# Reordering the first loads of a gated-recurrence layer, with fewer warm-up passes on TensorE

## The chip, the cores and the metric

The kernel runs on one core of one Trainium2 chip. The metric is the device time of one execution in microseconds (us); three runs of the kernel before gave 619.55, 619.95 and 620.02, median 619.95. Engines are named as in the profile: PE is the matrix engine (TensorE), with its weight loads shown apart as PEld; DVE is VectorE, ACT is ScalarE, POOL is GpSimd, and SP (SyncE) issues most of the DMAs. A suffix q (SPq, ACTq) marks an instruction of the engine's sequencer, such as the issue of a DMA.

## The reference

The input `x` has eight sequences of 1024 tokens with 256 channels. Each is normalized, goes through two branches, and both are added to it:

```python
xn = _layernorm(x)
# branch 1: gated linear recurrence, 384 channels
gate, u = xn @ Wg.T, xn @ Wi.T
y  = causal_depthwise_conv4(u) + conv_b
ig = sigmoid(y @ lru_Wi.T + lru_bi);  rg = sigmoid(y @ lru_Wg.T + lru_bg)
alpha = exp(-8 * softplus(lam) * rg);  beta = sqrt(1 - alpha**2 + 1e-6)
h  = associative_scan(h = alpha * h_before + beta * ig * y)
a  = (gelu(gate) * h) @ Wo.T
# branch 2: token-shifted feed-forward, 256 channels
xr, xk = mu * xn + (1 - mu) * xn_before      # one mu for r, one for k
f  = sigmoid(xr @ W_r.T) * (square(relu(xk @ W_k.T)) @ W_v.T)
out = x + a + f
```

Everything is float32.

## The kernel before

One sequence after the other goes through the core. A sequence is eight tiles of 128 tokens (`TT = 8`). Most products are done by a seven-product scheme of Strassen and Winograd: for it GpSimd forms sums of weight blocks (`weight_sum`, L408, tiles `sum_u`, `sum_k` and so on, once for the whole kernel) and sums of token blocks (`token_sum`, L803, tiles `xsum`, `side`, `rsum`, `ysum`, for every sequence). The products themselves are recorded at L415 (512 columns) and L421 or L830 (by token).

The order of instructions on every engine is written out by hand. `steps` collects calls with a due time, either given or from the table `PLACES`, and at the end they are issued in the order of these times. Nothing reorders them after that: each engine works through its own queue in order, and waits at an instruction until the semaphores that it needs are there. The head of the program, lines L1002 to L1087, stands ahead of that and is issued as written.

What the head does, in the order in which the steps follow from each other:

- The loads. SP issues `xt` (x of the first sequence) as four DMAs of two tiles each, 256 KB (`load`, L707). ACT issues the weights of u, `w_i`, 384 KB (`load_weight`, L349), then the parameters `par` (L1010), and loads its table for Sqrt (L1011). SP goes on with the other weights: `w_g` for the gate, which lies in the same tile `w_u`, then `w_k`, `w_r`, `lru_wg`, `lru_wi`, `w_v`, `w_o`.
- The DMAs of SP and ACT share eight semaphores in turn. A DMA waits until the one issued eight places before it has landed.
- `busy(15)`: fifteen matmuls on zeros (L1025, 128x512, bf16) that nothing reads. PE can do nothing else until they are through, since its queue is in order.
- Normalization of tiles 0 and 1: `sums_of_tiles` (L725) and `moments` (L729) on DVE, `deviation` (L732) on ACT, `inverse` (L739, L740) on DVE, and `normalize`, one tile on ACT (L749) and one on DVE (L747).
- `early_transposes(0)` (L1044): four transposes of 128x128 on PE into one bank; `early_put(0)` (L1057): ACT copies the bank into `xnT`. Then `busy(2)`, two more matmuls on zeros.
- The same for tiles 2 and 3, 4 and 5, 6 and 7, interleaved with the first products. These are u's first two row blocks, done plainly in quarters of 256 tokens (`plain_quarters`, L581): quarter f needs `xnT` of tiles 2f and 2f+1, so PE alternates between transposes of the next pair and products of the last.
- ACT's queue has `early_put(0)` ahead of `deviation` of tiles 2 and 3, so that deviation waits until PE has done the first transposes.
- POOL starts `weight_sum` for `sum_u` when `w_i` and `w_g` have landed, does the sums for r and k after it, and then the token sums of `xnT`, `xk` and `xr`.

After the head comes u's second group, then k, r, v and so on, each as seven products; the other seven sequences follow with PE as the engine that is always busy.

Of the kernel before, what the change touches and what calls it, by code (L numbers as in the profile page):

```python
# [9 lines left out]
AF = mybir.ActivationFunctionType  # L10
# [231 lines left out]
def kernel(  # L242
# [24 lines left out]
    nc = tc.nc  # L267
    B, S, D = x.shape
    TT = S // P
# [6 lines left out]
    def fixed(name, shape, dtype=F32):  # L276
        return const.tile([P] + shape, dtype, tag=name, name=name)


    par = fixed("par", [COLS])  # L280
# [57 lines left out]
    def take():  # L338
        return free.pop(0)

    def give(b):
        free.append(b)
# [4 lines left out]
    def load_weight(engine, name, src):  # L347
        family, first = ROWS[name]
        engine.dma_start(families[family][:, :, first * P : first * P + src.shape[2]], src)  # L349
# [356 lines left out]
    def load(s, t, n):  # L706
        nc.sync.dma_start(  # L707
            xt[:, t : t + n, :],
            x[s, t * P : (t + n) * P, :].rearrange("(t p) d -> p t d", p=P),
        )  # L710
# [8 lines left out]
    def stats(s, t, n):  # L719
        sums_of_tiles(s, t, n)  # L720
        moments(s, t, n)
# [279 lines left out]
    with tc.manual_schedule():  # L1001
# [1 line left out]
        nc.gpsimd.memset(ln_eps, LN_EPS)  # L1003
        nc.gpsimd.memset(beta_eps, BETA_EPS)
        make_identity(nc, ident)
        for t in range(0, TT, 2):
            load(0, t, 2)
            if t == 2:
                load_weight(nc.scalar, "i", w_i)
                nc.scalar.dma_start(par, params)  # L1010
                nc.scalar.preload_act_table(AF.Sqrt)  # L1011
        load_weight(nc.sync, "g", w_g)
        load_weight(nc.sync, "k", w_k)
        load_weight(nc.sync, "r", w_r)
# [7 lines left out]
        def busy(n):  # L1022
            for _ in range(n):
                b = take()
                nc.tensor.matmul(banks[b], warm[:, 0:P], warm, start=True, stop=True)  # L1025
                give(b)
# [40 lines left out]
                mu_rest, par[:, COL_MU_R : COL_MU_K + DC], -1.0, 1.0, ALU.mult, ALU.add  # L1067
            )

        busy(15)  # L1070
        stats(0, 0, 2)
        scales(0, 2)
        early_normalize(0)
# [289 lines left out]
```

## Time and profile before

| What | Value |
|---|---|
| Median of three runs | 619.95 us |
| The profiled execution's own time | 620.45 us |
| Its span, first to last instruction | 618.7 us |
| PE busy | 613.3 us (99%), 2539 instructions |
| DVE, ACT, POOL busy | 532.0, 472.7, 320.2 us (86%, 76%, 52%) |
| PE busy from 0 to 20 us | 18.07 us |
| PE busy from 20 to 200 us, and from 200 to 600 us | 179.60 us, 400.00 us |
| PEld idle in the first 20 us, by what ended it | ACT `xnT` (put) 1.4 us, `xt` (normalize) 1.7 us |

The profile is of one execution. A row of the timeline gives the start in us from the span's start, the duration in us, the engine, the line, the operation, the tiles and, in brackets, how long the engine stood idle before it and for whom. A row of the chain of waits gives a start, a duration and what held the program up then: the chain is followed back from the last instruction, at each step to what released it. "issue" is time in which an engine waited for nothing that the profile shows.

### The profile page before, as it was taken

The numbers are of one execution on the slowest core, as the hardware profiler recorded it, in microseconds if no ns is written. First come the engines' busy times: TensorE is split into PE (matmuls) and PEld (weight loads), VectorE is DVE, ScalarE is ACT, GpSimd is POOL, SyncE is SP. The second block draws the span as 40 slices with busy tenths as digits, with TensorE's granted clock in tenths as the row PEclk, the third lists the DMA queues.
The fourth block names the chain that finished last, engine by engine and source line by source line (L and its number), as shares of the span: only waits on it lengthen the run. The fifth ranks groups of instructions, "written<-read, shape, count | busy, mean of one in ns | idle before, by whom it ended". The sixth has DMA issues, their size and how long they took to land.

```text
span 618.7 us, 7488 instructions
## 1 busy us (share of the span) xinstructions
PE 613.3 (99%) x2539; PEld 370.0 (60%) x2539; DVE 532.0 (86%) x659; ACT 472.7 (76%) x671; POOL 320.2 (52%) x227
## 2 busy tenths in 40 slices
PE   8999999999999999999999999999999999999998
PEld 4575445954469544794448844497445964457466
DVE  5789799999989798898899888998888986789696
ACT  4988998668894788938889398884888749884880
POOL 4977923579034950549407492084911769427000
DMA  7200600164001810029000480006500044000403
GB/s 272 69 1 8 129 0 1 27 179 69 0 1 48 195 31 0 1 69 205 0 1 1 102 171 0 2 3 151 120 0 1 17 120 69 0 0 1 69 17 119
DMA packets 35478, 35.10 MB, mean 57 GB/s; under 512 B 2800, under 2 KB 34928, under 8 KB 35440
## 3 DMA queue, kind: packets, MB, share of 16 engines
q1 hardware_dynamic: 26416, 25.63, 14.9%
q0 software_dynamic: 8320, 8.39, 9.1%
q10 hardware_dynamic: 704, 0.60, 0.3%
q8 instruction: 20, 0.33, 0.2%
q14 instruction: 18, 0.15, 0.1%
HBM read 19.94 MB, written 8.39 MB: 46 GB/s over the span
## 4 chain that ended last, share of the span: by engine, by line
PE 96%; DVE 3%; issue 0%; ACT 0%; DVEq 0%
PE bank L415 65%; PE bank L421 24%; PE bank L830 4%; PE bank L1025 1%; PE bank L581 1%; DVE xr L820 1%; DVE xt L747 0%; DVE bank L499 0%; DVE st L725 0%; PE bank L754 0%; DVE q L915 0%; PE bank L1044 0%; DVE mv L740 0%; DVE q L930 0%; DVE mv L729 0%
## 5 line engine op out<-in xcount | busy, mean ns | idle before, releaser
L415 PE MATMUL bank<-y,w_l 128*128 128x512 f32 x288 | 138.2, 593 | 0.1
L898 DVE SCALAR_TENSOR_TENSOR y<-u,par,y 128x1024 f32<-128x1024 f32 x72 | 111.6, 1573 | 0.2
L491 ACT COPY bank<-bank 128x512 f32<-128x512 f32 x76 | 43.8, 576 | 61.3 <-PE bank L415 45.3
L415 PEld LDWEIGHTS bank<-y,w_l 128*128 128x128 f32 x288 | 52.9, 190 | 59.2 <-issue 56.9
L499 DVE TENSOR_TENSOR bank<-bank,five 128x512 f32<-128x512 f32 x76 | 52.3, 689 | 26.4 <-PE bank L415 25.6
L415 PE MATMUL bank<-ysum,sum_l 128*128 128x512 f32 x144 | 71.1, 594 | 0.2
L415 PE MATMUL bank<-xsum,sum_u 128*128 128x512 f32 x138 | 69.3, 592 | 0.0
L803 POOL TENSOR_TENSOR tr<-g 128x512 f32<-128x512 f32 x12 | 22.0, 1836 | 83.7 <-ACT u L611 69.8
L803 POOL TENSOR_TENSOR ysum<-y,ysum 128x512 f32<-128x512 f32 x16 | 28.4, 1777 | 53.6 <-DVE y L898 51.1
L803 POOL TENSOR_TENSOR xsum<-ysum 128x512 f32<-128x512 f32 x12 | 16.0, 1347 | 66.0 <-PE bank L421 58.8
L415 PEld LDWEIGHTS bank<-ysum,sum_l 128*128 128x128 f32 x144 | 26.8, 190 | 35.3 <-issue 28.7
L496 ACT COPY five<-bank 128x512 f32<-128x512 f32 x76 | 43.6, 583 | 4.9 <-PE bank L415 2.9
L415 PE MATMUL bank<-xnT,w_u 128*128 128x512 f32 x92 | 47.0, 592 | 0.0
L623 ACT ACTIVATE tr<-bank,half_b 128x512 f32<-128x512 f32 x48 | 32.0, 679 | 15.6 <-PE bank L415 15.6
L415 PEld LDWEIGHTS bank<-xsum,sum_u 128*128 128x128 f32 x138 | 25.7, 190 | 29.7 <-issue 27.5
L421 PE MATMUL bank<-w_o,g 128*128 128x128 f32 x288 | 37.0, 275 | 0.0
L623 ACT ACTIVATE ti<-bank,half_b 128x512 f32<-128x512 f32 x48 | 31.5, 683 | 7.1 <-PE bank L415 6.9
L421 PEld LDWEIGHTS bank<-w_o,g 128*128 128x128 f32 x288 | 35.0, 192 | 2.9 <-issue 2.9
L749 ACT ACTIVATE xt<-xt,mv,std 128x256 f32<-128x256 f32 x60 | 33.9, 596 | 1.5 <-DVE mv L740 1.5
L922 DVE SCALAR_TENSOR_TENSOR ti<-ti,y 128x1024 f32<-128x1024 f32 (+1 forms) x25 | 29.9, 1216 | 3.9 <-ACT ti L623 3.9
L803 POOL TENSOR_TENSOR ysum<-y 128x512 f32<-128x512 f32 x16 | 20.4, 1273 | 23.8 <-DVE y L898 20.1
L925 DVE SCALAR_TENSOR_TENSOR ti<-ti,q 128x1024 f32<-128x1024 f32 (+1 forms) x25 | 31.8, 1272 | 0.7
(165 smaller groups left out, 1480.3 us busy)
## 6 DMA issues: line engine op xcount, KB each, us to landing
side<-in_x_dram POOLq DMA_DIRECT2D x8, 1024.0 KB, 9.3
xt<-in_x_dram SPq DMA_DIRECT2D x28, 256.0 KB, 5.1
xnT<-xk SPq DMA_DIRECT2D x96, 64.0 KB, 2.0
out_dram<-side SPq DMA_DIRECT2D x12, 512.0 KB, 4.8
xt<-in_x_dram SPq DMA_DIRECT2D x1, 1024.0 KB, 5.3
out_dram<-side SPq DMA_DIRECT2D x4, 256.0 KB, 2.2
out_dram<-side SPq DMA_DIRECT2D x6, 128.0 KB, 1.8
w_l<-in_lru_wg_dram SPq DMA_DIRECT2D x1, 576.0 KB, 5.8
```

The costliest lines, as they stand in the source:

```text
L415: nc.tensor.matmul(banks[b], weight, tokens, start=start, stop=True, skip_group_check=True)
L421: nc.tensor.matmul(banks[b][:, p], tokens[:, p], weight, start=start and j == 0, stop=True, skip_group_check=True,)
L491: nc.scalar.copy(banks[bank["B"]], banks[bank["A"]])
L496: nc.scalar.copy(self.five, banks[bank["C"]])
L499: nc.vector.tensor_tensor(banks[bank["C"]], banks[bank["B"]], self.five, ALU.add)
L623: nc.scalar.activation(dst[:, m, HALVES[h]], src, AF.Tanh, bias=half_b[:, b + m : b + m + 1], scale=0.5)
L749: nc.scalar.activation(xa, xa, AF.Identity, bias=m, scale=r)
L803: nc.gpsimd.tensor_tensor(dst[o], a, b, ALU.subtract)
L830: nc.tensor.matmul(banks[b][:, j * D : (j + 1) * D], lhs[:, c, (t + j) * P : (t + j + 1) * P], families[w][:, c, :], start=(j == 0 and c = ...
L898: nc.vector.scalar_tensor_tensor(y[:, m, :], u[:, m, k : k + S], column(COL_CONV_W + k * HC + m), y[:, m, :], ALU.mult, ALU.add,)
L922: nc.vector.scalar_tensor_tensor(ti[:, m, p], ti[:, m, p], 1.0, y[:, m, p], ALU.add, ALU.mult)
L925: nc.vector.scalar_tensor_tensor(ti[:, m, p], ti[:, m, p], 0.5, q[:, m, p], ALU.mult, ALU.mult)
```

## The change

In the head, all loads but the parameters go to SP. Tiles 0 and 1 come as two DMAs of 128 KB in place of one of 256 KB, the weights `w_i` of u come third, then the three other pairs of tiles, then the other weights in the order that they had. ACT loads its Sqrt table first and issues the parameters after that. The warm-up passes ahead of the first transposes become eleven in place of fifteen; the two after the transposes stay.

```diff
-        for t in range(0, TT, 2):
+        nc.scalar.preload_act_table(AF.Sqrt)
+        load(0, 0, 1)
+        load(0, 1, 1)
+        load_weight(nc.sync, "i", w_i)
+        for t in range(2, TT, 2):
             load(0, t, 2)
-            if t == 2:
-                load_weight(nc.scalar, "i", w_i)
-                nc.scalar.dma_start(par, params)
-                nc.scalar.preload_act_table(AF.Sqrt)
+        nc.scalar.dma_start(par, params)
         load_weight(nc.sync, "g", w_g)
         load_weight(nc.sync, "k", w_k)
         load_weight(nc.sync, "r", w_r)
...
-        busy(15)
+        busy(11)
         stats(0, 0, 2)
         scales(0, 2)
         early_normalize(0)
```

Nothing else differs. The engines' queues keep their order from the first transposes on; the banks that the products use are shifted by four places, and the semaphores of the DMAs by one.

## The prediction

> **What bounds the kernel now.** I read the page first: PE is busy 99% of the span.
>
> ```profile
> PE 613.3 (99%) x2539; PEld 370.0 (60%) x2539; DVE 532.0 (86%) x659; ACT 472.7 (76%) x671; POOL 320.2 (52%) x227
> ```
>
> In the stretches, PE is busy 400.00 us of 200 to 600 and 18.07 us of 0 to 20. So a gain in the head counts as far as PE's continuous run begins earlier, and no other engine then comes late for it. Next I read the chain of waits of the first 60 us.
>
> ```profile
> 1.18 5.96 PE bank L1025 x15
> 7.14 0.45 PE bank L1044 x4
> ...
> 8.10 0.31 ACT std L732
> ...
> 8.82 0.98 DVE xt L747
> ...
> 10.70 0.94 DVE mv L740
> 11.64 0.16 DVE mv L729 x2
> 11.79 1.06 DVE xt L747
> 12.85 0.04 issue
> 12.90 0.55 PE bank L1044 x3
> 13.44 1.81 PE bank L581 x8
> 15.25 0.44 PE bank L1044 x4
> 15.69 2.67 PE bank L581 x12
> 18.36 13.73 PE bank L415 x32
> ```
>
> The reader should see three stretches: the warm-up passes hold the start to 6.98 (where the first transpose begins), then a chain of DVE and ACT for normalizing holds PE until 12.90, and from there PE runs without a gap through the plain quarters to 18.36. Last, the timeline of DVE, ACT and POOL.
>
> ```profile
> 5.22 0.41 DVE L747 TENSOR_SCALAR xt<-xt,std,mv 128x256 f32<-128x256 f32 x1
> 5.96 0.75 DVE L725 BATCH_NORM_STATS2 st<-xt 128x6 f32<-128x256 f32 x2 [0.33 <-DMA xt<-in_x_dram]
> 6.85 0.72 DVE L725 BATCH_NORM_STATS2 st<-xt 128x6 f32<-128x256 f32 x2
> ...
> 5.22 0.60 ACT L749 ACTIVATE xt<-xt,mv,std 128x256 f32<-128x256 f32 x1 [0.43 <-DVE mv L740]
> ...
> 8.65 2.01 POOL L408 TENSOR_TENSOR sum_u<-w_u 128x384 f32<-128x384 f32 x2 [7.21 <-DMA w_u<-in_w_g_dram]
> 10.62 0.99 POOL L408 TENSOR_TENSOR sum_u<-sum_u,w_u 128x384 f32<-128x384 f32 x1
> 11.70 1.00 POOL L408 TENSOR_TENSOR sum_u<-w_u,sum_u 128x384 f32<-128x384 f32 x1
> ```
>
> Tiles 0 and 1 are ready at 5.22 + 0.60 = 5.82, so the transposes wait 1.16 us for warm-ups. And DVE's 256-wide operations, 0.41 us at 5.22, take 0.98, 0.94 (a 2-wide one, 0.16 at 5.02) and about 1.1 us once POOL runs: each ends 0.03 to 0.14 us after an operation of POOL ends (9.66, 11.61, 12.70). While POOL runs, such an operation costs what is left of POOL's.
>
> **The change, step by step.** *Four passes fewer.* Weight loads of warm-ups start every 0.43 us up to 6.27, then at 6.55 and 6.76: the twelfth starts at 5.85. After eleven, the transposes can start at 5.85 in place of 6.98: 1.13 us earlier, hidden by nothing, since the data is there at 5.82. But the pitch falls to 0.21 only at about 6.4, so PE's clock has not risen when the eleven are through; the four transposes, 0.60 us before, may take up to twice that, and I take 0.25 us more.
>
> [...]
>
> *The loads.* By the packet records of the trace, the order in which bytes moved was already x0-1, w_i (first packet at 2.69, though ACT issued it at 0.73), x2-3 (mostly from 3.7), and the new order is the same. One SP issue of 256 KB takes 0.5 us, of 384 KB 0.69 (w_g). So after: tile 0 at 0.73, tile 1 at about 1.2, w_i at about 1.7, x2-3 at 2.4, x4-5 at 2.9, x6-7 at 3.4, w_g at 3.9 where it was 2.75. From issue to first packet the first load took 1.1 us (0.73 to 1.82), so w_i can move at 2.8 and x2-3 at 3.5: I expect the landings to stay (x0-1 3.40, w_i 5.23, x2-3 5.94, x4-5 6.73, x6-7 7.46, w_g 8.51), within -0.4 to +0.7 us; the far end is w_g's issue-to-landing of 5.8 us with its issue 1.1 us later, half of it made up. Two single tiles land tile 0 up to 0.4 us earlier, worth nothing while the eleven passes last until 5.85; if tile 1 came 0.4 us later, that cover would be gone and it would cost the excess.
>
> The later SP issues are all behind more than 2 us of queued bytes. `w_k` waits for tile 0's landing, `lru_wi` for `par`; `par` (first read at 13.64, landed at 6.15) may be 0.6 us later: nothing. ACT's table load of 1.28 us moves from 2.06 to 0.73, nothing, since ACT's first use is at 4.49.
>
> *What follows on the chain.* ACT's put of pair 0 (7.62) comes at 6.75; the next deviation can start at 7.2 (8.10). DVE is through the sums of tiles 4 and 5 at 6.85 + 0.72 = 7.57, so the reciprocal starts at 7.6 (8.43), and DVE's normalization of tile 3 at 8.0, ahead of POOL's start at 8.65, so it takes 0.41, not 0.98: end 8.41 (9.80), with ACT's tile 2 at 8.6 (9.42). The second transposes go at 8.65 (9.48, held up to 9.86). Sums of tiles 6 and 7 and a reciprocal (0.87 us by the row of 9.73 to 10.59) put the 2-wide `mv` operation at 9.30 (10.70). It ends with POOL's first operation, at 9.7 (11.64); normalization of tile 5 ends with POOL's second, at 10.75 (12.84). So the third transposes are ready at 10.75; PE has the second transposes (0.44), two quarters (8 x 0.223 = 1.78, with put 1 through at 9.86) until 10.87. From there it needs 5 quarters x 0.892 + 2 x 0.44 = 5.35 us: the quarters end at 16.2, where they ended at 18.36. Normalization of tile 7 ends with POOL's fourth operation, 12.84 at worst, and is wanted at 13.1.
>
> That is 2.1 us. *Does it reach the end?* POOL's weight sums still start at 8.65 and end at 15.69; the first token sum takes 1.30, so it is there at 17.0, where PE now wants it at 16.2 + 0.86 = 17.1 (17.69 and 19.05 before). POOL is 0.7 us earlier, PE 2.1: all later deliveries of POOL lose 1.4 us of slack. They have: 2.2 (second sum, 20.31 against 22.5), 2.2 (`side`, 23.76 against 25.92), 2.0 and more to 33.3, where POOL itself waited 1.23 us for DVE, which follows PE. The tightest is `rsum` at 36.73 against 37.15. I take 0.1 us off for such places: a gain of 2.0 us. On the profiled execution, 620.45 - 2.0 = 618.45; that lies 0.50 above the median, so against the median 617.95.
>
> **The rivals.** *One POOL slot missed (gain 1.0).* If the chain is 0.36 us later, the `mv` operation misses the end of POOL's first operation at 9.66 and ends at 10.65, and tile 5 at 11.75; PE's run starts at 11.9 in place of 12.9: 618.95. For it: the second `mv` before did just that. [...] Against: 0.36 us of margin.
>
> *The loads come later (no gain).* If x2-3 lands 0.65 us later, DVE's tile 3 starts after POOL's 8.65 and ends at 9.80 as before; the rest is as before: 619.95. For it: SP now issues what two queues did, and x2-3's issue moves from 1.23 to 2.4. Against: x2-3's packets moved from 3.7 only.
>
> [...]
>
> *It does not do what it says:* moving w_i to SP does nothing for its landing; I hold that likely and it is in the sum.
>
> **The numbers.** Full gain (617.5 to 618.5): 0.55. One slot missed (618.6 to 619.3): 0.27. No gain: 0.10. Slower: 0.08. A measurement of this kernel tells 0.2% from no change, about 1.24 us, so faster means below 618.71 and slower above 621.19. The first case and a quarter of the second are faster: 0.62; most of the slower case stays within 0.2%, so slower 0.05, same 0.33. The range from 617.4 to 619.4 takes in the first two cases.
>
> **What would show it.** First transposes (L1044) at 5.8 to 5.9; the third group at 10.8 to 11.0 (one slot missed: 11.9); the first L415 at about 16.2; warm-up pitch, and whether L581 passes come at 0.22 or 0.45 us; POOL's first weight sum at 8.6 to 8.8; no new PE wait for `xsum` at 17 or for `rsum` at 35. I am wrong if POOL starts after 9.4, if the sums of tiles 2 and 3 start after 6.5, or if PE gains in the head and gives it back at a POOL delivery.

## The result, and the profile after

The changed kernel takes 622.04 us (median of six runs, 621.22 to 622.97) where the kernel before takes 619.59 (six runs beside it, 619.29 to 620.02): a ratio of 1.0039, 95% interval 1.0029 to 1.0049. The change loses 2.45 us where 2.0 were forecast to be won. The profiled execution took 622.67 us, span 620.9. The six runs lie in two groups: three at 621.22 to 621.41, where TensorE's mean granted clock is 1.000, and three at 622.67 to 622.97, where it is 0.997.

Timeline of PE in the kernel after (start, duration, what; in brackets the idle time before and for whom):

```profile
5.86 1.06 PE L1045 MATMUL bank<-ident,xt 128*128 128x128 f32 x4
8.92 0.66 PE L1045 MATMUL bank<-ident,xt 128*128 128x128 f32 x4 [0.20 <-ACT xt L749]
11.22 0.60 PE L1045 MATMUL bank<-ident,xt 128*128 128x128 f32 x4
...
16.57 1.02 PE L415 MATMUL bank<-xnT,w_u 128*128 128x512 f32 x2
19.84 1.12 PE L415 MATMUL bank<-xsum,sum_u 128*128 128x512 f32 x2 [2.25 <-POOL xsum L803]
20.80 1.86 PE L415 MATMUL bank<-xnT,w_u 128*128 128x512 f32 x2
22.45 1.91 PE L415 MATMUL bank<-xsum,sum_u 128*128 128x512 f32 x2
24.15 1.08 PE L415 MATMUL bank<-xnT,w_u 128*128 128x512 f32 x2
25.07 1.02 PE L415 MATMUL bank<-xsum,sum_u 128*128 128x512 f32 x2
```

The reader should see two things. Up to 16.57 the change does what was forecast: the first seven-product multiplication (L415) starts 1.62 us earlier than before (18.19). Then PE does one pair of products and stands idle for 2.25 us, since POOL has not delivered `xsum`. Before, the same two pairs followed each other without a gap:

```profile
18.19 1.02 PE L415 MATMUL bank<-xnT,w_u 128*128 128x512 f32 x2
19.05 1.02 PE L415 MATMUL bank<-xsum,sum_u 128*128 128x512 f32 x2
```

In the kernel after, two further rows are slow: pairs that take 1.02 us at 16.57 and 25.07 take 1.86 and 1.91. The stretches of the same profile say why (each row: from and to, length, then the busy time of PE, PEld, DVE, ACT and POOL, the granted clock, and the DMAs' share and GB/s):

```profile
17.50:20.90 3.40, 1.15 (x4) 0.59 (x4) 2.32 (x6) 1.07 (x2) 3.40 (x4) 0.99 0.37 131
20.90:24.35 3.45, 3.45 (x6) 1.39 (x5) 0.44 (x2) 2.25 (x4) 3.45 (x4) 0.51 0.00 0
24.35:27.80 3.45, 3.45 (x10) 1.54 (x9) 1.21 (x3) 3.11 (x5) 3.45 (x4) 1.00 0.00 0
```

PE was busy for 1.15 us of the first stretch; in the next one it works without a gap, at half the clock. By the clock records of the trace the half clock lasts from 20.85 to 24.27, which by itself makes some 1.7 us (half of 3.4). So the profiled execution roughly adds up: 1.62 won in the head, 2.25 lost waiting, 1.7 lost to the clock, 2.3 lost in all, where the spans differ by 620.9 - 618.7 = 2.2. It is a rough sum: at L421 PE is 2.58 us behind (34.51, before 31.93), and some 0.4 us of that is caught up later. The three executions without the lowered clock are 1.5 us shorter.

Why `xsum` is late is in the chain of waits of the kernel after (start, duration, what held the program up):

```profile
4.03 5.46 DMA w_u<-in_w_g_dram
9.49 0.02 issue
9.51 0.02 POOLq L408
9.53 0.10 issue
9.63 2.97 POOL sum_u L408 x3
...
16.18 1.40 POOL sum_k L408
17.58 2.21 POOL xsum L803
19.79 0.04 issue
19.84 14.84 PE bank L415 x30
```

Before, this chain went through the warm-ups and the normalization. Now it goes from the issue of `w_g` to its landing, through POOL's eight weight sums, to `xsum`. Timeline of POOL and DVE, kernel before and then kernel after:

```profile
15.24 0.45 POOL L408 TENSOR_TENSOR sum_k<-w_k,sum_k 128x128 f32<-128x128 f32 x1
16.39 1.30 POOL L803 TENSOR_TENSOR xsum<-xnT 128x512 f32<-128x512 f32 x1 [0.70 <-ACT xnT L1057]
17.57 3.82 DVE L820 SCALAR_TENSOR_TENSOR xk<-xnT,par,xk 128x1024 f32<-128x1024 f32 x2 [3.45 <-ACT xk L814]
```

```profile
8.27 0.41 DVE L747 TENSOR_SCALAR xt<-xt,std,mv 128x256 f32<-128x256 f32 x1
...
9.57 0.16 DVE L740 SCALAR_TENSOR_TENSOR mv<-mv,std 128x2 f32<-128x2 f32 x1
9.63 2.00 POOL L408 TENSOR_TENSOR sum_u<-w_u 128x384 f32<-128x384 f32 x2 [8.19 <-DMA w_u<-in_w_g_dram]
...
15.95 2.71 DVE L820 SCALAR_TENSOR_TENSOR xk<-xnT,par,xk 128x1024 f32<-128x1024 f32 x2 [2.23 <-ACT xk L814]
16.13 1.44 POOL L408 TENSOR_TENSOR sum_k<-w_k,sum_k 128x128 f32<-128x128 f32 x1
17.54 2.24 POOL L803 TENSOR_TENSOR xsum<-xnT 128x512 f32<-128x512 f32 x1
```

POOL starts 0.98 us later than before (8.65). And DVE's mixing of `xk`, which PE's earlier transposes let start at 15.95 instead of 17.57, now lies ahead of POOL's last sums: `sum_k` takes 1.44 us where it took 0.45, `xsum` 2.24 where it took 1.30. The three delays, 0.98 + 0.99 + 0.94 = 2.9 us, put `xsum` at 19.8 instead of the forecast 17.0.

### The profile page after: what moved, and what is told of

It is laid out like the page before. It is cut to its first block, busy times and chain, and to the rows that moved or that the text cites. A ratio compares the mean times of both kernels' runs of the same rounds, so it can differ in the third digit from the quotient of the medians.

```text
span 620.9 us, 7482 instructions
## 1 busy us (share of the span) xinstructions
PE 613.9 (99%) x2535; PEld 370.6 (60%) x2535; DVE 529.0 (85%) x659; ACT 472.7 (76%) x671; POOL 320.4 (52%) x227
## 4 chain that ended last, share of the span: by engine, by line
PE 94%; DVE 2%; POOL 2%; DMA 1%; SPq 0%; issue 0%; DVEq 0%; POOLq 0%
PE bank L415 65%; PE bank L421 24%; PE bank L830 4%; DMA w_u<-in_w_g_dram 1%; POOL sum_u L408 1%; DVE xr L820 1%; POOL sum_k L408 0%; SPq L707 0%; POOL xsum L803 0%; DVE bank L499 0%; PE bank L754 0%; DVE q L915 0%; DVE st L725 0%; POOL sum_r L408 0%; DVE q L930 0%
## 5 line engine op out<-in xcount | busy, mean ns | idle before, releaser
L415 PE MATMUL bank<-y,w_l 128*128 128x512 f32 x288 | 138.1, 593 | 0.0
L415 PEld LDWEIGHTS bank<-y,w_l 128*128 128x128 f32 x288 | 52.9, 190 | 58.9 <-issue 56.4
L415 PE MATMUL bank<-xsum,sum_u 128*128 128x512 f32 x138 | 70.3, 600 | 2.2 <-POOL xsum L803 2.2
L415 PE MATMUL bank<-ysum,sum_l 128*128 128x512 f32 x144 | 71.1, 594 | 0.2
L415 PEld LDWEIGHTS bank<-ysum,sum_l 128*128 128x128 f32 x144 | 26.8, 190 | 35.2 <-issue 28.7
L415 PE MATMUL bank<-xnT,w_u 128*128 128x512 f32 x92 | 47.9, 602 | 0.0
L415 PEld LDWEIGHTS bank<-xsum,sum_u 128*128 128x128 f32 x138 | 25.9, 192 | 32.8 <-issue 27.6
L421 PE MATMUL bank<-w_o,g 128*128 128x128 f32 x288 | 37.0, 275 | 0.0
L421 PEld LDWEIGHTS bank<-w_o,g 128*128 128x128 f32 x288 | 35.0, 192 | 2.9 <-issue 2.9
```

The source lines that it names most:

```text
L415: nc.tensor.matmul(banks[b], weight, tokens, start=start, stop=True, skip_group_check=True)
L421: nc.tensor.matmul(banks[b][:, p], tokens[:, p], weight, start=start and j == 0, stop=True, skip_group_check=True,)
```

## The experiments

The runs e1 to e18 were made in five groups, each on one chip with the kernel before beside it; the ratios hold within a group. The medians of before in the five groups are 620.18, 620.16, 619.29, 619.53 and 620.13, so microseconds are not compared across groups. "POOL" is the start of the first weight sum, "L415" that of the first seven-product multiplication, "idle" PE's wait for an `xsum` in the products after it, all from the profiled execution.

| Run | Ratio to before (95%) | POOL | L415 | idle |
|---|---|---|---|---|
| before (profiled) | 1 | 8.65 | 18.19 | none |
| after | 1.0039 (1.0029 to 1.0049) | 9.63 | 16.57 | 2.25 |
| e7_after_again | 1.0025 (1.0011 to 1.0040) | 10.38 | 16.88 | 2.83 |
| e1_loads_15 | 1.0010 (1.0000 to 1.0020) | 9.38 | 16.96 | none |
| e2_old_loads_11 | 0.9994 (0.9986 to 1.0003) | 8.21 | 16.07 | none |
| e11_old11_again | 0.9998 (0.9990 to 1.0007) | 8.60 | 16.33 | none |
| e3_fill | 1.0017 (1.0008 to 1.0026) | 9.67 | 18.85 | none |
| e4_pool_order | 1.0007 (0.9998 to 1.0016) | 9.64 | 17.09 | none |
| e10_xsum_three_earlier | 1.0011 (1.0001 to 1.0021) | 9.96 | 16.62 | 0.85 |
| e8_wg_early | 0.9996 (0.9988 to 1.0005) | 7.67 | 17.36 | none |
| e9_wg_before_last | 1.0011 (1.0003 to 1.0020) | 9.11 | 17.51 | none |
| e5_wi_by_act | 1.0011 (1.0003 to 1.0020) | 8.80 | 18.49 | none |
| e12_wi_by_act_second | 1.0002 (0.9994 to 1.0011) | 9.47 | 17.16 | none |
| e6_pair | 1.0007 (0.9999 to 1.0016) | 9.51 | 16.96 | 0.85 |
| e13_par_late | 1.0017 (1.0006 to 1.0027) | 9.38 | 16.83 | 0.86 |
| e14_old11_par_first | 1.0004 (0.9995 to 1.0013) | 9.89 | 17.38 | none |
| e15_pair_par_late | 1.0009 (1.0000 to 1.0018) | 9.24 | 16.83 | none |
| e16_old11_singles | 1.0014 (1.0005 to 1.0022) | 8.25 | 17.94 | none |
| e17_old11_rsum_early | 1.0109 (1.0092 to 1.0126) | 8.88 | 16.62 | 5.35 for `w_v` |
| e18_pool_order_rsum_early | 1.0108 (1.0093 to 1.0123) | 9.77 | 17.22 | 5.19 for `w_v` |

### The two halves of the change apart

e1 is after with `busy(15)`; e2 is before with `busy(11)`; e7 and e11 run after and e2 once more, unchanged.

```diff
 # e1, against after
-        busy(11)
+        busy(15)
 # e2 and e11, against before
-        busy(15)
+        busy(11)
```

> The changed kernel's loads with the fifteen warm-up passes of before. Theory A (the order of the loads delivers the gate weights 1.0 us late, POOL starts at 9.63 in place of 8.65, and its first token sum comes late for PE): POOL starts at 9.5 to 9.7 here too; PE wants the first xsum at about 19.0, POOL has it between 18.0 and 19.8, so PE waits 0 to 0.8 us and the clock is not lowered: 619.6 to 620.5. Rival B (the eleven passes are the cause, the loads do nothing): 619.6 with POOL's start at 8.65.

> The loads of before with eleven warm-up passes in place of fifteen. Theory A: POOL starts at 8.65, weight sums end at 15.7, the first xsum is there at 17.0 to 17.9 and PE wants it at 17.1 to 17.4: a wait under 0.8 us, no lowered clock, 617.6 to 618.9. Rival B (eleven passes let PE and DVE run ahead of POOL, and DVE's mixing of xk holds POOL up): PE waits for xsum more than 1.5 us, 620.5 or more.

> The changed kernel once more, on the same chip as the others. POOL starts at 9.3 to 9.7; PE waits more than 1.5 us for the first xsum in most executions; 621 to 623, with the mean clock at 0.997 in those above 622.

> The loads of before with eleven passes, once more on another chip, to see whether its 0.7 us are there again: 0.3 to 1.2 us below the kernel before in the median; POOL starts at 8.1 to 8.7, no wait of PE for xsum above 0.5 us.

e1's time came out as theory A has it, with a median of 620.29 and no wait. The others missed in their times: e2's median is 619.49, above the expected 617.6 to 618.9; e7's is 620.78, below the expected 621, with eight of its twelve executions at 619.39 to 621.20 and four at 622.73 to 624.36; e11's lies 0.10 us below before, where 0.3 to 1.2 were expected.

The chain of waits of e2:

```profile
5.89 0.64 PE bank L1044 x4
...
8.42 0.66 PE bank L1044 x4
9.07 1.81 PE bank L581 x8
...
16.23 13.73 PE bank L415 x32
29.96 1.78 PE bank L421 x16
```

The profile of e2 runs through the head as the prediction wrote it: first transposes at 5.89 (5.85), quarters to an end at 16.23 (16.2), no wait for `xsum` behind, span 617.0, which is 1.7 us below before's 618.7. Of the 2.12 us won at the first L415 (16.07 against 18.19), 0.4 are given back by the last L421 group ahead of L830 (40.08 against 41.79). So the eleven passes are good for most of what was said of them in that execution; the loads take it away and more. But neither e2 nor e11 is measurably faster than before over all their runs. e1 shows what that is about: it has all fifteen passes, and its first L415 is at 16.96, 1.23 us earlier than in the profile of before. There POOL starts at 9.38, after DVE's normalization of tile 3 (8.67, 0.41 us). Part of the 2.1 us forecast was thus not held by the passes but by POOL's start in the one execution that was profiled. e7 repeats the loss, with POOL even later; e1's loss is smaller, since PE comes at 17.82 for an `xsum` that is there at 17.62.

### The lowered clock

e3 gives PE eight passes on zeros in the gap, so that it is not idle while `xsum` is late.

```diff
 # e3, against after
                     quarters(f, 1)
+                pe(busy, 8, length=0)
                 us[1].step(1)
```

> The changed kernel with eight more warm-up passes between the last plain quarter and the first product of u's second group, so that PE is busy for 1.7 us of the 2.25 us that it waits for xsum; the wait itself stays. If the lowered clock of about 3.4 us that follows the wait (0.50 in the profile) costs what separates the runs near 622.9 from those near 621.3, all runs are at 621.2 to 621.6 with a mean clock of 1.000. If the clock has nothing to do with the idle time, runs at both levels stay.

Measured 620.83 (620.10 to 622.17): better than expected, with mean clock 0.999 or 1.000 in all eleven runs, where three of six runs of after and four of twelve of e7 had 0.997. Its one run above 622 is at 1.000, so that one is slow for a reason that is not known. Its profile has no idle time of PE there. That fits a clock lowered by the idle time: with PE kept busy it stayed. After was not in the same group, so the size of the gain (0.0022 or 0.0008 in the ratio, by which run of after one takes) is uncertain. The wait for `xsum` need not be the only thing that lowered the clock: 0.997 also stands beside three of eleven executions of e16, whose profile shows no such wait, and one each of e1, e5 and e13. None of these executions was profiled, so which idle time was at work there is open.

### POOL's order

```diff
 # e4, against after, in PLACES: two xsum ahead of the weight sums of k and r
-        "early weight_sum k 0 False": 5.75,
-        "early weight_sum k 2 False": 6.13, "early weight_sum k 1 False": 6.5,
-        "early weight_sum r 1 False": 6.87, "early weight_sum k 3 False": 7.18,
-        "early token_sum x 1": 10.53,
+        "early weight_sum k 0 False": 7.6,
+        "early weight_sum k 2 False": 7.61, "early weight_sum k 1 False": 7.62,
+        "early weight_sum r 1 False": 7.64, "early weight_sum k 3 False": 7.63,
+        "early token_sum x 1": 7.55,
 # e10, against after: one xsum ahead of the last three weight sums
-        "early weight_sum k 1 False": 6.5, "early weight_sum r 1 False": 6.87,
-        "early weight_sum k 3 False": 7.18,
+        "early weight_sum k 1 False": 7.51, "early weight_sum r 1 False": 7.52,
+        "early weight_sum k 3 False": 7.53,
```

> The changed kernel with POOL's order changed: the first two token sums of xnT go ahead of the weight sums of k and the last two of r, which PE wants only from 24 us on. Theory A (PE waits because xsum stands behind weight sums that started 1.0 us late): xsum starts when the last put is through, at 14.7, and is there at 16.0, ahead of PE's 17.4; no wait, clock 1.000, 617.6 to 618.4. If something else takes the gain (k's sums then late for PE at 24 to 25 us, or the clock), 619.5 or more.

> The changed kernel with the first token sum three places earlier in POOL's queue, ahead of the last three weight sums of k and r (1.3 us of work). Theory A with its second part (a late POOL meets DVE's mixing of xk, which starts at 15.95, and its operations then take 1 us more): xsum starts at 15.3 to 15.5, before the mixing, takes 1.3 us in place of 2.24 and is there at 16.6 to 16.8, ahead of PE's 17.4; no wait, no lowered clock; POOL's later deliveries (rsum near 37) are 0.3 to 1 us late in place: 619.0 to 620.5. Without that second part xsum gains only its 1.3 us and PE still waits about 1 us: 620.5 to 621.5.

Both take the wait at the first `xsum` away, and neither brings the forecast back: e4 took 620.49 where 617.6 to 618.4 was expected, e10 620.05, inside its range. In e10 the first `xsum` begins at 15.71, ahead of DVE's mixing of `xk` at 16.00, and takes 1.30 us again; the next one is late by 0.85 us. In e4 the lateness goes on; its chain of waits:

```profile
15.29 1.31 POOL xsum L803
...
26.29 2.22 POOL side L803
...
34.68 2.27 POOL rsum L803
36.95 0.04 issue
36.99 2.05 PE bank L421 x16
```

From the first `xsum` to `rsum` at 36.95 the chain is POOL's nearly all the way: what is put behind there is missing later. e17 (on e2) and e18 (on e4) then tried to free POOL ahead of `rsum`, by moving the halving of `w_v` and one weight sum behind it.

```diff
 # e17, against e2, and e18, against e4
-        "early halve v": 22.98, "early weight_sum l 0 False": 24.71,
+        "early halve v": 35.9, "early weight_sum l 0 False": 33.69,
```

> The loads of before, eleven passes, and on POOL the halving of w_v (1.49 us) and the first weight sum of the gates (0.99 to 1.66 us) moved from ahead of the second rsum to behind the last rsum, where POOL stood idle for 3.77 us. Theory 1 (POOL's work up to rsum at about 37 us takes back what the eleven passes gain): POOL reaches the second and third rsum about 2 us or more ahead of PE, ratio 0.9970 to 0.9985, clearly below the 0.9994 and 0.9998 of eleven passes alone. Theory 2 (in most executions the gain is lost earlier, at the landing of w_g and the first normalizations): ratio 0.9990 to 1.0000 as without the move.

> After (the new loads, eleven passes) with the two first xsum ahead of the weight sums of k and r, as in e4_pool_order, and with the halving of w_v and the first weight sum of the gates behind the last rsum. Theory 1: the wait of PE for rsum at 37 us is gone, what is left is the wait for side at 25 us (1.1 us in e4_pool_order): ratio 0.9985 to 0.9998, where e4_pool_order had 1.0007. Theory 2: 1.000 to 1.001 as there. In both, no lowered clock and no execution above 622.

Timelines of POOL and of PE in e17:

```profile
32.65 2.18 POOL L803 TENSOR_TENSOR rsum<-xr,rsum 128x512 f32<-128x512 f32 x1 [2.32 <-DVE xr L820]
...
46.70 9.93 PE L830 MATMUL bank<-w_v,ysum 128*128 128x256 f32 x32 [5.35 <-POOL w_v L394]
```

The move was a mistake: PE reads the halved `w_v` directly in the products at L830, due at 41.3, so it waits 5.35 us, and the ratio says nothing of either theory. What the traces do show is small. In e17 the second `rsum` waits 2.32 us for DVE's `xr`, so most of POOL's freed time goes unused, and the last `rsum` starts at 37.01 where e2 has it at 37.20 (in e18 at 38.01, in e4 at 39.11). From the first L415 to the last L421 group ahead of L830, PE takes 23.60 us in e17 against 24.01 in e2, and 24.22 in e18 against 24.91 in e4; before took 23.60, so up to there e17 keeps all that it won in the head. POOL's order up to `rsum` is thus worth 0.4 to 0.7 us in these executions, a part of what is missing and not all of it.

### Why the loads are late

In these runs parts of the loads are changed one at a time.

```diff
 # e5, against after: w_i by ACT, as its first DMA
+        load_weight(nc.scalar, "i", w_i)
         nc.scalar.preload_act_table(AF.Sqrt)
...
-        load_weight(nc.sync, "i", w_i)
 # e6, against after: tiles 0 and 1 as one DMA
-        load(0, 0, 1)
-        load(0, 1, 1)
+        load(0, 0, 2)
 # e9, against after (e8 makes the same move in e2): w_g ahead of tiles 6 and 7
+            if t == 6:
+                load_weight(nc.sync, "g", w_g)
             load(0, t, 2)
...
-        load_weight(nc.sync, "g", w_g)
 # e12, against after: par, then w_i, by ACT behind its table
         nc.scalar.preload_act_table(AF.Sqrt)
+        nc.scalar.dma_start(par, params)
+        load_weight(nc.scalar, "i", w_i)
...
-        load_weight(nc.sync, "i", w_i)
...
-        nc.scalar.dma_start(par, params)
 # e13, against after, and e15, against e6: par by SP behind w_g
-        nc.scalar.dma_start(par, params)
         load_weight(nc.sync, "g", w_g)
+        nc.sync.dma_start(par, params)
 # e14, against e2: par ahead of w_i
+                nc.scalar.dma_start(par, params)
                 load_weight(nc.scalar, "i", w_i)
-                nc.scalar.dma_start(par, params)
 # e16, against e2: tiles 0 and 1 as two DMAs, then the other pairs
+        load(0, 0, 1)
+        load(0, 1, 1)
+        for t in range(2, TT, 2):
-        for t in range(0, TT, 2):
```

> The changed kernel with w_i issued by ACT at the very start again, ahead of ACT's table load and the parameters; the rest, single tiles and eleven passes, as changed. Theory A (w_i behind two other loads on SP leaves the DMA engines part empty from 2.8 to 4.0 us, and SP issues w_g 1.3 us later): no such dip, w_g is issued at 3.3, lands at 8.1 to 8.6, POOL starts at 8.2 to 8.7, and the time is that of the old loads with eleven passes, 0 to 1 us below before. Rival C (the single tiles do it): dip stays, POOL starts at 9.4 or later, time above before.

> The changed kernel with tiles 0 and 1 in one DMA again, all loads but the parameters still by SP. Theory A: w_i is issued at 1.24 in place of 1.64 and its first packet comes at 2.7 in place of 3.1; about half of the dip is gone, POOL starts at 9.0 to 9.4, and PE still waits for xsum, 0.8 to 1.8 us: 620.5 to 621.5. Rival C (single tiles): POOL starts at 8.2 to 8.7, the time is 0 to 1 us below before.

> The loads of before and eleven passes, with w_g issued ahead of the last pair of tiles, so that POOL can start some 0.7 us earlier. Theory A says that POOL's chain from the landing of w_g to the second rsum at 37 us is what bounds the head once PE is earlier: POOL starts at 7.5 to 7.9 and the time is 0.5 to 1 us below the old loads with eleven passes, 1 to 2 us below before. If PE's own chain bounds (the last pair lands later, or DVE's normalizations now stand behind POOL from 7.7), no gain over eleven passes alone: 0 to 1 us below before.

> The changed kernel with w_g issued ahead of the last pair of tiles: all loads still by SP, the stream as a whole still behind, only POOL's weights half a microsecond further forward in it. Theory A (what costs time is POOL's start): w_g is issued at 3.5, POOL starts at 8.7 to 9.1, the first xsum is there at 17.0 to 17.9, PE waits under 0.8 us and the clock stays: 619.0 to 620.3, no execution above 621.5. If the all-SP stream hurts mainly in another way (tiles 2 and 3 late), 620.5 to 622 as for the changed kernel.

> The changed kernel with w_i issued by ACT right after the parameters, so behind the first single tile and beside the second, and not by SP. Theory A: no dip in the stream, 1806 KB are through at 7.2 to 7.8 (8.2 in the changed kernel), POOL starts at 8.2 to 8.8; tile 1 lands before 4.0, so the first transposes go at 5.6 to 6.0; time 0.3 to 1.5 us below the kernel before. If w_i again passes tile 1 (as when ACT issued it first, tile 1 at 5.13), first transposes at 7 or later and 620 to 621.

> After, with the parameters issued by SP behind w_g instead of by ACT at 0.76; all other loads as in after. Theory P (the parameters' 128 small packets, moved at 2.0 to 2.8, put the whole stream back): 1806 KB are through at 7.3 to 7.5 in place of 8.1 to 8.3, w_g lands at 8.5 to 9.0, POOL starts below 9.1, no wait of PE for xsum above 0.5, ratio 0.998 to 0.9995. Theory Q (the loads are behind because SP issues them one after the other, w_i at 1.64 and w_g at 4.03): 1806 KB at 8.1 to 8.3, POOL at 9.4 to 9.7, ratio 1.001 to 1.004. Theory S (the two single tiles): as Q here.

> The loads of before with eleven passes, but ACT issues the parameters ahead of w_i. Theory P: the stream falls behind though SP's order is the old one, 1806 KB at 7.9 to 8.3 and POOL's start at 9.0 or later, ratio above that of eleven passes alone by 0.001 or more. Theories Q and S: the stream is as in before, 1806 KB at 7.2 to 7.5, POOL at 8.2 to 8.7, ratio 0.999 to 1.000.

> After with tiles 0 and 1 as one DMA of 256 KB and the parameters issued by SP behind w_g: only w_i's place on SP is left of the change to the loads. Theory P: 1806 KB at 7.2 to 7.4, POOL below 8.9, ratio 0.998 to 0.9995. Theory Q: 1806 KB at 8.0 to 8.3, POOL at 9.3 to 9.6, ratio about 1.001. Theory S: 7.2 to 7.4, as P, but then the run with single tiles and late parameters is behind.

> The loads of before with eleven passes, but tiles 0 and 1 as two DMAs of 128 KB, so that SP's later issues move by the 0.4 to 0.5 us of one more issue. Theory S: 640 KB at 4.6 or later and 1806 KB at 8.0 or later. Theories P and Q: 640 KB at 4.0 to 4.3, 1806 KB at 7.2 to 7.6, POOL at 8.3 to 9.0. First transposes at 5.85 in all cases, ratio 0.999 to 1.001.

From the packet records, the time in us at which the packets begun by SP's and ACT's queues together came to so many KB (640 is tiles 0, 1 and `w_i`; 1806 is as much as `xt`, `w_i`, the parameters and `w_g` together), and when `w_g` was issued and had landed:

| Run | who issues w_i | par's packets | 640 KB | 1806 KB | w_g issued, landed |
|---|---|---|---|---|---|
| before | ACT | late | 3.98 | 7.35 | 2.75, 8.51 |
| e2 | ACT | late | 3.95 | 7.20 | 2.75, 8.07 |
| e14 | ACT | early | 4.27 | 7.53 | 2.77, 9.75 |
| e16 (singles) | ACT | middle | 4.02 | 7.40 | 3.21, 8.11 |
| e12 (singles) | ACT, behind par | early | 4.59 | 7.77 | 3.14, 9.33 |
| after (singles) | SP | early | 4.86 | 8.21 | 4.03, 9.49 |
| e6 | SP | early | 4.42 | 8.24 | 3.62, 9.36 |
| e13 (singles) | SP | late | 4.57 | 8.14 | 4.03, 9.24 |
| e15 | SP | late | 4.54 | 8.18 | 3.62, 9.10 |

This settles which part puts the stream behind, as theory Q has it. All eleven profiles with `w_i` on SP, after among them, have 1806 KB at 8.11 to 8.43; the nine with `w_i` on ACT, before among them, at 7.20 to 7.79. The single tiles (e16) and the early parameters (e14) don't put the stream behind when `w_i` stays with ACT, and taking both out of after (e15) leaves it behind. That SP issues `w_g` later is not enough by itself either: e16 issues it 0.46 us later than e2 and has it at the same time. What is left is `w_i` in SP's row. The stretches of the profiles show where the bytes are missing: in the two half microseconds from 3.0 to 4.0 the DMAs moved 95 and 98 GB/s in after and 142 and 249 in e15, where they moved 347 and 343 in before and 325 and 345 in e16. Why the lag of e15 on before grows from 0.56 us at 640 KB to 0.83 at 1806 KB is not settled by these runs.

For the time this settles less. e6 and e15 keep `w_i` on SP and stand at 1.0007 and 1.0009, where e7, in e6's group, has 1.0025 (their intervals overlap). Tenths of a microsecond decide there, since POOL's late start meets DVE's mixing of `xk`. In e1 and e15 `xsum` begins 0.02 and 0.04 us ahead of the mixing (16.33 and 16.17) and takes 1.29. In e6 and e13 it begins 0.12 and 0.11 us behind it and takes 2.32 and 2.33, and PE waits 0.85. In after `sum_k` is behind it too, both are lengthened, and PE waits 2.25.

Landing has a tail besides. In the traces a load reports in sixteen parts, and POOL starts behind the last of them. In e14 the first part of `w_g` was in at 7.57 and fifteen at 8.12, but the last at 9.75, so POOL began at 9.89 although the stream was on time. So e14 has the stream of theories Q and S and the late POOL of theory P. In e2 all sixteen came within 0.5 us, in before and after within 1.1, in e7 within 2.2.

e5 and e16 have a fault of their own: `w_i` by ACT, issued at once, overtakes tile 1, which is then SP's second DMA (landed at 5.13 in e5). In e16 tile 1 lands at 4.76, the first transposes go at 6.95, and L415 begins at 17.94. e12 avoids that, with `w_i` on ACT behind the parameters, and is the best of the versions of after (0.9994 to 1.0011); it was expected 0.3 to 1.5 us below before, but `w_g` landed only at 9.33. e5 was expected below before too, and e6 at 620.5 to 621.5, where it took 619.99; e8 (619.77) and e9 (620.16) lie in the ranges given for them. e8 brings POOL forward, to 7.67, and shows the other side; DVE's timeline:

```profile
7.75 0.93 DVE L740 SCALAR_TENSOR_TENSOR mv<-mv,std 128x2 f32<-128x2 f32 x1
8.72 1.05 DVE L747 TENSOR_SCALAR xt<-xt,std,mv 128x256 f32<-128x256 f32 x1
```

POOL, begun early, now lies in the way of tile 3 (the same two rows take 0.16 and 0.41 us in after), and L415 begins 1.3 us later than in e2. e9 trades the same way on after: `w_g` earlier, tiles 6 and 7 at 9.63, L415 at 17.51.

No version is measurably faster than before: the intervals of e2, e8 and e11, the lowest three, all hold 1.

## Why the prediction was wrong, point by point

- *Four passes fewer*: right. The transposes started at 5.86 (forecast 5.85). They took 1.06 us where 0.85 was allowed; the clock record shows full speed from 7.20, and the plain quarters behind them had their pace of before (eight passes of L581 in 1.97 us in both). The early start was in part luck: by the pace of the same passes the clock came up at about 4.0 in e4, 4.8 in e2 and 6.4 in the profile of before. Where it comes early, the passes are not what holds the start: in e2 they end at 5.52 and the transposes begin at 5.89.
- *The chain on DVE, ACT and PE*: right in kind, and 0.35 us late because tiles 2 to 7 came 0.3 to 0.9 us later. Tile 3 took 0.41 us at 8.27, the `mv` operation escaped POOL altogether, third transposes at 11.22 (10.87), first L415 at 16.57 (16.2).
- *"I expect the landings to stay"*: this is the step that failed. `w_g` landed at 9.49, 0.98 us later, outside the stated far end of +0.7. The reason given was that the order of bytes stays the same and that SP's later issues are hidden behind queued bytes. The order did stay; the pace did not, as soon as `w_i` stood in SP's row (e13, e15): 1806 KB were through at 8.21 in place of 7.35.
- *"POOL's weight sums still start at 8.65 and end at 15.69; the first token sum takes 1.30"*: failed with it. Besides the late start, durations of before were carried over to a time in which DVE does something else: 0.45 became 1.44, and 1.30 became 2.24. In these profiles the first `xsum` takes 1.29 to 1.30 us where it begins ahead of DVE's mixing of `xk` (e1, e10, e15), and 2.24 to 2.33 us where it begins behind the start of it (after, e6, e13); the cause is not shown by these runs.
- *The slack*: the prediction had `xsum` at 17.0 and wanted at 17.1. A bound of +0.7 us on `w_g` was written down and not carried on to this place, where there was 0.1 us of slack. It would have given a rival with a wait at `xsum`, on the slower side. Instead the slack was priced at 0.1 us for all of POOL; e2, with the old loads and no wait for `xsum`, gives back 0.4 by the last L421 group.
- *The rivals*: "the loads come later" named the right event, but looked for its effect at tile 3, where lateness of `w_g` helped (its normalization on DVE took 0.41 us in after, 1.05 in e8 with POOL at 7.67), and not at `xsum`. A slower kernel was given 0.08; it came by the wait for `xsum`, and in three of the six executions by a lowered clock besides (a mean of 0.997).
- *The time before*: the gain was taken against the profiled execution and then subtracted from the median. Of the 33 runs of before in the first group, 12 took 618.79 to 619.68 and 20 took 620.06 to 620.54, and the profiled one, with 620.45, belongs to the upper ones. e2's lowest run, 618.76, is the lowest of before, 618.79. So a gain worked out against that profile need not exist for the others. That before's faster executions are those in which POOL starts after tile 3 would fit e1, but none of them was profiled, and it stays open.
- The sign itself: the prediction said it would be wrong if POOL started after 9.4 or if PE gained in the head and gave it back at a POOL delivery. Both happened (POOL at 9.63; 1.62 us won by the first L415 and lost at `xsum`).

## What to carry to other kernels

When a chain is made shorter, reckon the deliveries of the engines beside it again with the new overlaps, and take each stated bound to the place with the least slack: 0.1 us of slack and a bound of 0.7 us is a rival. Moving a load to another issuing engine was here a change of pace, not only of order (1806 KB at 8.21 in place of 7.35); look at which landing starts the longest chain of a slow engine before giving up a second issuer. And a forecast against one profiled execution holds for that execution: where runs of the same kernel lie a microsecond apart, ask first which of them the profile is.

## What was not expected of the hardware

- *The clock was halved after an idle time of 2.25 us.* After 2.25 us without work (2.83 in e7, 5.35 in e17) PE was granted half the clock, in after from 20.85 to 24.27, in e7 for about 3.4 us from 21.2, so 1.0 and 0.4 us after PE had work again; in the profiles, waits of 0.85 us (e6, e10, e13) were not followed by it (mean clock 0.999 or 1.000). It cost 1.5 us in after, where it came in three of six executions, and in four of twelve of e7.

The stretches of e17 around its longer wait, columns as above:

```profile
41.30:46.70 5.40, 0.05 (x2) 0.01 (x1) 5.36 (x4) 5.22 (x7) 5.34 (x3) 0.89 0.00 0
46.70:48.30 1.60, 1.60 (x4) 1.32 (x5) 1.57 (x5) 1.60 (x4) 0.00 (x0) 0.50 0.00 0
48.30:51.70 3.40, 3.40 (x10) 2.65 (x9) 3.03 (x4) 0.27 (x1) 0.00 (x0) 0.50 0.00 0
51.70:55.10 3.40, 3.40 (x16) 2.95 (x15) 0.00 (x0) 0.00 (x0) 2.14 (x2) 0.91 0.00 0
```

The clock goes down while PE waits (0.89 is a mean over the wait) and stays at 0.50 for 5.6 us after PE has work again: to 51.70, and by the mean of 0.91 for some 0.6 us of the last stretch.

- *The issuing engine mattered.* `w_i` on SP instead of ACT put 1806 KB of loads 0.3 to 1.2 us later (8.11 to 8.43 against 7.20 to 7.79).
- *The parameters were not held by the table load ahead of them.* ACT's table load ran from 0.73 to 2.0, and the parameters behind it were issued at 0.76 and landed at 3.17, where the prediction expected them no earlier than before (6.15).
